# First places of runs by DRAM as a 123rd row of the rank product, and ScalarE's sort comparisons 22 places ahead of their scatters

## The chip, the cores and the metric

One core of a Trainium2 chip runs the whole program in one launch. The metric is the device time of one execution in microseconds. Besides the timed runs there is one execution with a profile; its trace carries every instruction of the engines TensorE (PE, with its weight loads PEld), VectorE (DVE), ScalarE (ACT) and GpSimd (POOL), and the DMAs that SP and the others issue.

## The reference

A layer of a graph network on 6,250 nodes of 128 features with 206,250 edges. The edges' features are added up by the edge's source node, and the sums go through three small layers and a normalization:

```
edge_aggr = zeros(n, 128).at[src].add(edge_attr)
combined  = concat([x, edge_aggr, global], -1) @ W_c + b_c
h   = softplus(combined @ W1 + b1)
h   = softplus(h @ W2 + b2)
out = layernorm(x + h @ W3 + b3)
```

Nearly all of the work is the sum by node, `.at[src].add`: the edges come in no order of `src`.

## The kernel before

**Sort, scatter, sum.** The nodes are cut into 32 buckets of 196. The edges lie as 122 partitions (`PN`) by 1,692 columns, two columns to a pair: 846 pairs. The program (1) sorts each column's 122 edges by bucket with a product of a 0/1 matrix (`sort_hot`) and the edges' rows (`gather`, TensorE, line 1153), (2) copies the result from PSUM to `pairs` (`settle`, ScalarE, 1165), (3) scatters one pair of columns per indirect DMA into `rows_by` in DRAM (`scatter_row`, GpSimd, 1182), where each bucket has a room of its own, (4) loads full chunks of 128 rows back (`load`, SP), makes 0/1 matrices of them against the 196 nodes (`match`, VectorE, 990) and multiplies them with the rows (`product`, TensorE, 1013), and adds that to `sums_t` (`add`, VectorE, 1036). When all is summed, the node layers follow (`node_layers`, lines 1340 on).

**Positions.** To sort a column, each edge needs its slot: the first place of its bucket's run in the column, and its rank within the run. To scatter, each sorted pair needs its row in `rows_by`. `positions(g)` computes both for one of eight groups of pairs (`GROUPS`: 28, 72, 124, 124, 124, 128, 124, 122), in sets of 16 columns, and sets in batches of up to four. A set has four quads of four columns. By step: `count_set` (VectorE, 498) makes the 0/1 tile `pair_ib` (edge by bucket and column); `counted` (TensorE, 509) counts the runs; `even_set` (520); `evened` (TensorE, 527) sums the counts up to the first places; `started` (VectorE, 534 to 538) takes them out of PSUM, as float32 (`starts`) and as a bfloat16 copy (`starts_h`); `ranked` (TensorE, 557 and 559) makes the slots; `slot_set` (VectorE, 576) reduces them to `slot`. `ranked` is one product of the 122 x 122 constant `rank` with `pair_ib` (512 columns), and then four products, one per quad, that add the first places: `starts_h` broadcast over 122 columns against the identity. From group 5 on (`GAP`), a group's positions come in two parts, counts first, ranks and rows a group later (`split`).

**What sets the order.** Nothing is scheduled by the machine: each engine runs its instructions in the order in which the program emits them, and that order is a list of events sorted by a planned time. A scatter is planned every 1.3 us (`SCATTER`) from 24 us on; a piece of three pairs is compared 17.5 ahead of its first scatter (`COMPARED`), gathered 14 ahead and settled 10.5 ahead. Even pieces are compared by VectorE in one instruction (1137), odd pieces by ScalarE in seven: six times `Abs` (1140) and one `Relu` over all (1142), half a place apart, and these begin another `SPREAD` (2.0) earlier. Rows of edges are loaded 36 ahead. The steps of `positions` are spread evenly over 85% of the time of the group before (`at_step` numbers them; `APART` is 3). All of SP's DMAs, loads of rows, loads of chunks and the fills of `rows_by`, are one queue (`sync_dma`, line 293), and SP waits in it for whatever the next DMA waits for.

The few lines that matter most here:

```
def rank(k, at, t):
    at_step(at, (1, lambda t=t: ranked(t)))
    at_step(at + APART, (0, lambda t=t: slot_set(t)))
...
for j in range(2 * pieces[i][2] + 1):
    when(t - COMPARED - SPREAD + j * SCATTER / 2, lambda i=i: compare_next(i))
```

## Time and profile before

| | |
|---|---|
| timed runs, us | 1288.87, 1288.93, 1285.73; median 1288.87 |
| the profiled execution, us | 1289.92 |
| its span, first to last instruction, us | 1288.2 |
| granted TensorE clock, mean | 0.962 |
| scatters on GpSimd | 846, from 22.1 to 1127.0 us |
| sort products and sum products on TensorE | 3384 and 3516 rows of the trace |
| packets of all DMA queues | 381.96 MB, 297 GB/s |

The span of the profiled execution lies 1.7 us under its time; the rest is ahead of the first and behind the last instruction. A product of float32 data is one instruction of the program and two rows of the trace. A duration of a product in a row reaches from its start to its modelled end, and products overlap; the distance of two starts is what one costs. "<-" in a wait names what ended last before the waiting instruction could start.

### The profile page before, as it was taken

The page shows a single profiled execution, that of the slowest core. Times are in us where ns is not written, and L with a number is a line of the kernel's source. Part 1 is how long each engine was busy: PE and PEld are TensorE (multiplying, and loading weights), DVE is VectorE, ACT ScalarE, POOL GpSimd, SP SyncE. Part 2 cuts the span into 40 slices and gives each one's busy share as a digit, 9 for nine tenths or more (in the row PEclk, how much of TensorE's full clock was granted, in tenths as well). Part 3 has the DMA queues.
Part 4 walks back from the last instruction along what each step waited for, and adds up shares of the span by engine and source line. Part 5 has one row for each costly group of instructions (what it writes and reads, how often), then busy time and mean ns, then how long its engine had stood idle before and what let it go on. Part 6 is the DMA issues. An engine that isn't in the chain of part 4 may idle for free.

```text
span 1288.2 us, 26304 instructions
## 1 busy us (share of the span) xinstructions
PE 1167.7 (91%) x8617; PEld 1111.8 (86%) x8617; DVE 1027.6 (80%) x2260; ACT 1003.9 (78%) x2335; POOL 880.9 (68%) x915
## 2 busy tenths in 40 slices
PE   5778898888998998999899999999999999899893
PEld 5667788877988898989899999999999999898772
DVE  7868977888789977899878887789876767687784
ACT  5897987899687888977998888988899999403343
POOL 2777777777577776776777777777777777750334
PEclk9788998989999998999999999999999999999996
DMA  6789998899999997997999999999999999874421
GB/s 248 240 296 347 344 334 288 305 344 355 339 327 331 362 330 278 319 325 246 322 309 309 323 336 328 345 313 335 316 350 334 369 336 363 288 218 140 140 75 53
DMA packets 174636, 381.96 MB, mean 297 GB/s; under 512 B 27546, under 2 KB 118626, under 8 KB 160670
## 3 DMA queue, kind: packets, MB, share of 16 engines
q1 hardware_dynamic: 130751, 260.70, 61.2%
q0 software_dynamic: 41328, 115.65, 23.1%
q10 hardware_dynamic: 2415, 3.85, 0.9%
q8 instruction: 72, 1.18, 0.4%
q14 instruction: 70, 0.57, 0.1%
HBM read 242.47 MB, written 142.20 MB: 299 GB/s over the span
## 4 chain that ended last, share of the span: by engine, by line
PE 65%; DVE 12%; ACT 8%; DMA 7%; issue 4%; POOL 3%; SPq 0%; ACTq 0%; DVEq 0%; POOLq 0%
PE part L1013 37%; PE sorted L1153 21%; ACT pairs L1165 4%; DMA rows_by<-pairs,pair 4%; POOL rows_by L1182 3%; ACT sort_hot L1140 3%; DMA chunks<-rows_by 3%; DVE hot L990 2%; DVE past L727 1%; PE small L557 1%; PE small L559 1%; ACT sort_hot L1142 1%; DVE sort_hot L1137 1%; DVE sums_t L1036 1%; PE small L1395 1%
## 5 line engine op out<-in xcount | busy, mean ns | idle before, releaser
L1182 POOL DMA_INDIRECT rows_by<-pairs,pair x846 | 828.1, 979 | 298.3 <-issue 202.8
L1013 PE MATMUL part<-hot,chunks 128*128 128x196 f32 x3516 | 675.1, 335 | 13.2 <-DVE sums_t L1036 9.9
L1165 ACT COPY pairs<-sorted 64x387 f32<-64x387 f32 (+2 forms) x1144 | 542.6, 474 | 118.8 <-PE sorted L1153 95.7
L1013 PEld LDWEIGHTS part<-hot,chunks 128*128 128x128 f32 x3516 | 582.0, 193 | 21.9 <-DVE sums_t L1036 11.3
L1153 PE MATMUL sorted<-rows,sort_hot 122*128 122x129 f32 x3384 | 498.5, 288 | 44.5 <-ACT sort_hot L1142 32.0
L1153 PEld LDWEIGHTS sorted<-rows,sort_hot 122*128 122x128 f32 x3384 | 457.6, 199 | 53.5 <-ACT sort_hot L1142 36.3
L990 DVE TENSOR_TENSOR hot<-chunks,both_ps 128x784 f32<-128x784 f32 (+3 forms) x541 | 426.1, 809 | 9.2 <-DMA chunks<-rows_by 9.0
L1140 ACT ACTIVATE sort_hot<-plain,slot 122x128 f32<-122x128 f32 x840 | 292.8, 394 | 18.6 <-PE sorted L1153 6.3
L1036 DVE TENSOR_TENSOR sums_t<-sums_t,part 128x392 f32<-128x392 f32 (+1 forms) x262 | 143.5, 548 | 134.0 <-PE part L1013 133.0
L1137 DVE TENSOR_TENSOR sort_hot<-slot,both_ps 122x768 f32<-122x768 f32 x143 | 134.5, 940 | 1.9 <-PE sorted L1153 1.0
L1142 ACT ACTIVATE sort_hot<-sort_hot 122x768 f32<-122x768 f32 x143 | 118.6, 830 | 3.9
L1437 POOL TENSOR_SCALAR y<-y,mv,rs 128x128 f32<-128x128 f32 x40 | 31.1, 785 | 93.8 <-DVE rs L1425 93.5
L576 DVE TENSOR_REDUCE slot<-small 122x16 f32<-122x512 f32 (+2 forms) x109 | 72.9, 668 | 21.5 <-PE small L559 20.7
L1367 ACT ACTIVATE away<-sorted,z_bias 128x512 f32<-128x512 f32 (+2 forms) x13 | 8.5, 656 | 72.9 <-PE sorted L1357 72.9
L498 DVE TENSOR_TENSOR pair_ib<-pair_block,plain 122x512 bf16<-122x512 bf16 (+2 forms) x157 | 63.4, 411 | 0.2
L557 PE MATMUL small<-pair_ib,half 122*122 122x512 bf16 (+2 forms) x109 | 43.3, 398 | 7.6 <-DVE slot L576 7.5
L742 PEld LDWEIGHTS <-past 128*128 128x128 f16 x424 | 25.4, 100 | 17.9 <-DVE past L727 12.7
L727 DVE TENSOR_TENSOR past<-both_ps,starts 128x512 f16<-128x512 f32 (+1 forms) x61 | 39.8, 664 | 1.2 <-PE small L742 0.9
L742 PE MATMUL small<-jump,past 128*128 128x56 f16 (+3 forms) x424 | 29.4, 190 | 11.8 <-DVE past L727 8.4
L559 PEld LDWEIGHTS <-starts_h 128*122 128x122 bf16 x236 | 25.3, 148 | 11.9 <-issue 7.7
L1114 ACT COPY rows<-pair_i 122x16 f32<-122x16 f32 x106 | 22.2, 209 | 17.0 <-DMA rows<-in_edge 16.4
L727 DVE TENSOR_TENSOR past<-both_ps,starts_late 128x512 f16<-128x512 f32 (+2 forms) x49 | 32.3, 661 | 0.0
(163 smaller groups left out, 515.6 us busy)
## 6 DMA issues: line engine op xcount, KB each, us to landing
rows<-in_edge SPq DMA_DIRECT2D x105, 1032.0 KB
chunks<-rows_by SPq DMA_DIRECT2D x362, 136.0 KB
chunks<-rows_by SPq DMA_DIRECT2D x203, 204.0 KB
chunks<-rows_by SPq DMA_DIRECT2D x75, 272.0 KB
rows_by<-pairs,pair POOLq DMA_INDIRECT x846
rows_by<-fill SPq DMA_DIRECT2D x10, 1249.5 KB
rows_by<-fill SPq DMA_DIRECT2D x10, 714.0 KB
chunks<-rows_by SPq DMA_DIRECT2D x13, 408.0 KB
```

The costliest lines, as they stand in the source:

```text
L498: nc.vector.tensor_tensor(ib, cols.unsqueeze(2).to_broadcast([PN, m, SB, QUAD]), bucket_at[:PN].unsqueeze(1).to_broadcast([PN, m, SB, QUAD ...
L576: nc.vector.tensor_reduce(to, of, axis=mybir.AxisListType.X, op=ALU.max)
L727: nc.vector.tensor_tensor(past[:, :, a:b], twice_ps[:KB].unsqueeze(1).unsqueeze(1).to_broadcast([KB, 2, b - a, P // 2]), own["starts"][:, ...
L990: nc.vector.tensor_tensor(hot[:, q - a:q - a + m], chunks[j][:, lo:hi + 1:step, D:W].to_broadcast([P, m, BL]), iota_ps.unsqueeze(1).to_bro ...
L1013: nc.tensor.matmul(part[:, b - base_of[v], :], t[:, place_in(j, q), :D], hot[:, q - a], start=first, stop=last)
L1036: nc.vector.tensor_add(here, here, of)
L1137: return [lambda: nc.vector.tensor_tensor(hot[:PN, :2 * m], slot[:PN, at:at + 2 * m].unsqueeze(2).to_broadcast([PN, 2 * m, P]), slot_ps[:P ...
L1140: return [lambda j=j: nc.scalar.activation(hot[:PN, j], by_slot[:PN], AF.Abs, bias=slot[:PN, at + j:at + j + 1], scale=-1.0) for j in rang ...
L1142: for j in range(2 * m)] + [lambda: nc.scalar.activation(hot[:PN, :2 * m], hot[:PN, :2 * m], AF.Relu, bias=1.0, scale=-1.0)]
L1153: nc.tensor.matmul(out[:, j, :], hot[:PN, at], rows_at[col // LOAD_COLS][:PN, col % LOAD_COLS, :], start=True, stop=True)
L1165: nc.scalar.copy(sets_at[i][64 * n:64 * n + 64, lo:lo + m, h, :W], out[64 * h:64 * h + 64, :m, :])
L1182: s = nc.gpsimd.indirect_dma_start(out=dst, out_offset=bass.IndirectOffsetOnAxis(ap=at, axis=0), in_=rows[:, j].rearrange("p a b -> p (a b ...
```

## The change

**The first places.** In groups 2 to 7 (`rowed`: from `ROWED` = 2 on) the four products by which `ranked` added the first places are gone. `pair_ib` has a 123rd partition, the constant `rank` a 123rd row of ones, and the rank product runs over 123 rows: whatever stands in row 122 of `pair_ib` is added to every slot of that bucket and column. To get the first places into that one row, `evened` makes one more product per batch that puts them with quads on partitions (up to 16 x 128), `started` copies that to SBUF as `starts_rows` (in place of the copy `starts_h`) and writes it to a DRAM tensor of the group, and `starts_row` reads, for each set, four quads of it as one row of 512 values into `pair_ib`. The write is at step 9 of a batch as `started` was; in groups 2 to 4 the read is at step 16 and the rank product at 22 in place of 15, and a batch of n sets takes 10n steps in place of 8n. In groups 5 to 7 the read stands where `count_set` stands in the second part, three steps ahead of the rank product. Counts and first places of a batch lie closer together in PSUM, so that the new product has room.

**The comparisons.** `SPREAD` is 4.5 in place of 2.0, so that ScalarE's part of the comparisons is planned 22 ahead of the scatter. The pool of `sort_hot` has four buffers in place of three, that of the matches (`hots`) five in place of six.

The core of the diff:

```diff
-GAP = 5
+GAP, ROWED = 5, 2
-SHARE, SPREAD = 2, 2.0
+SHARE, SPREAD = 2, 4.5
-    t["rank"] = MARK * (k == f) + (f > k)
+    t["rank"] = MARK * (k == f) + (f > k) + (k == PN)
+    rows_of = {g: dram.tile([2 * (s1 - s0) // QUAD, KB], BF16, name=f"starts{g}")
+               for g, (s0, s1) in enumerate(groups) if g >= ROWED}
-    hots = ctx.enter_context(tc.tile_pool(name="hots", bufs=6))
+    hots = ctx.enter_context(tc.tile_pool(name="hots", bufs=5))
-        sort_p = phase.enter_context(tc.tile_pool(name="sort", bufs=3))
+        sort_p = phase.enter_context(tc.tile_pool(name="sort", bufs=4))
-        rank_h = rank_h[:PN, :PN]
+        rank_h = rank_h[:PN + 1, :PN]
-            split = g >= GAP
+            split, rowed = g >= GAP, g >= ROWED
-                ib = pairs_in.tile([PN, STEP // QUAD, SB, QUAD], BF16, name="pair_ib", bufs=5)[:, :m]
+                ib = pairs_in.tile([PN + 1, STEP // QUAD, SB, QUAD], BF16, name="pair_ib", bufs=5)[:, :m]
...
                 for k, by in enumerate((lower_h, through_h, lower_or_all_h)):
-                    nc.tensor.matmul(small_of["counts", ts][:KB, (1 + k) * P:(1 + k) * P + n], by,
+                    a = SPAN + (1 + k) * BATCH * STEP // QUAD
+                    nc.tensor.matmul(small_of["counts", ts][:KB, a:a + n], by,
                                      own["evens"][:, at], start=True, stop=True)
+                if rowed:
+                    nc.tensor.matmul(small_of["counts", ts][:n, P:P + KB], own["evens"][:, at],
+                                     lower_h, start=True, stop=True)
...
-                nc.vector.tensor_copy(own["starts_h"][:, at], small[:, 1, :n])
+                if not rowed:
+                    nc.vector.tensor_copy(own["starts_h"][:, at], small[:, 1, :n])
+                    return
+                rows_h = per.tile([BATCH * STEP // QUAD, KB], BF16, name="starts_rows", bufs=2)
+                nc.vector.tensor_copy(rows_h[:n], small_of["counts", ts][:n, P:P + KB])
+                sync_dma(rows_of[g][at], rows_h[:n])
+
+            def starts_row(t):
+                q0, n = t // QUAD, per_set(t)
+                sync_dma(in_set[t][PN:PN + 1].rearrange("p q b c -> p (q b c)"),
+                         rows_of[g][q0:q0 + n].rearrange("(o q) k -> o (q k)", o=1))
...
-                nc.tensor.matmul(pr, rank_h, in_set.pop(t)[:, :, :NB, :], start=True, stop=False)
+                k = PN + rowed
+                nc.tensor.matmul(pr, rank_h[:k], in_set.pop(t)[:k, :, :NB, :], start=True, stop=rowed)
+                if rowed:
+                    return
                 for q in range(per_set(t)):
...
                     at_step(base + 4 * k, (6, lambda t=t: count_set(t)))
+                    if rowed and not split:
+                        at_step(base + gap + 16 + 5 * k, (2, lambda t=t: starts_row(t)))
                     if not split:
-                        rank(k, base + gap + 5 * APART + 5 * k, t)
+                        rank(k, base + gap + (22 if rowed else 5 * APART) + 5 * k, t)
...
-                base += (4 if split else 8) * n
+                base += (4 if split else 10 if rowed else 8) * n
...
                     at_step(4 * n, (6, lambda t=t: count_set(t)))
+                    at_step(4 * n, (7, lambda t=t: starts_row(t)))
                     rank(n, 4 * n + APART, t)
```

How the instructions stand now, at three places.

ScalarE in group 3, from the comparisons of one odd piece (the `Abs` and the `Relu` into one `sort_hot`) to the copies of that piece's sorted pairs (into `pairs1`). Before, the comparisons into `sort_hot_4449`:

```order
L1140 ACTIVATE sort_hot_4449<-plain_60,slot_2025 122x128 x2
L1165 COPY pairs5_113<-sorted_4423 64x3x129 x2
L1140 ACTIVATE sort_hot_4449<-plain_60,slot_2025 122x128 x2
L1114 COPY rows_4279<-pair_i_114 122x16
L1140 ACTIVATE sort_hot_4449<-plain_60,slot_2025 122x128
L1165 COPY pairs5_113<-sorted_4444 64x3x129 x2
L1140 ACTIVATE sort_hot_4449<-plain_60,slot_2025 122x128
L1142 ACTIVATE sort_hot_4449<-sort_hot_4449 122x768
L1165 COPY pairs0_108<-sorted_4474 64x3x129 x2
L1165 COPY pairs0_108<-sorted_4501 64x3x129 x2
L1140 ACTIVATE sort_hot_4549<-plain_60,slot_2025 122x128 x2
L1165 COPY pairs1_109<-sorted_4513 64x3x129 x2
```

And now the same piece, into `sort_hot_4334`:

```order
L1167 ACTIVATE sort_hot_4334<-plain_60,slot_1999 122x128 x3
L1192 COPY pairs4_118<-sorted_4318 64x3x129 x2
L1167 ACTIVATE sort_hot_4334<-plain_60,slot_1999 122x128 x3
L1192 COPY pairs5_119<-sorted_4346 64x3x129 x2
L1169 ACTIVATE sort_hot_4334<-sort_hot_4334 122x768
L1141 COPY rows_4217<-pair_i_120 122x16
L1192 COPY pairs5_119<-sorted_4366 64x3x129 x2
L1192 COPY pairs0_114<-sorted_4383 64x3x129 x2
L1167 ACTIVATE sort_hot_4434<-plain_60,slot_1999 122x128 x3
L1192 COPY pairs0_114<-sorted_4408 64x3x129 x2
L1167 ACTIVATE sort_hot_4434<-plain_60,slot_1999 122x128 x3
L1192 COPY pairs1_115<-sorted_4436 64x3x129 x2
```

Between the last step of the comparisons and the first copy of their own piece stood four copies and two comparisons of the next piece; now there are six copies, six comparisons and a copy of nodes.

TensorE in group 1, where the positions of group 2 are made, from the first batch's last product of first places to its first rank product (into `small` from `pair_ib`). Before:

```order
L527 MATMUL small<-evens,half 128x16
L1153 MATMUL sorted<-rows,sort_hot 128x129 x6
L557 LDWEIGHTS half
L557 MATMUL small<-pair_ib,half 122x512
L559 LDWEIGHTS starts_h
L559 MATMUL small<-half,starts_h 122x128
```

And now:

```order
L531 MATMUL small<-evens,half 128x16
L534 LDWEIGHTS evens
L534 MATMUL small<-half,evens 16x128
L1180 MATMUL sorted<-rows,sort_hot 128x129 x9
L579 LDWEIGHTS half
L579 MATMUL small<-pair_ib,half 122x512
L1180 MATMUL sorted<-rows,sort_hot 128x129 x3
```

Nine products of the sort stand between the two in place of six, and the four products of `starts_h` behind the rank product are gone.

SP in group 3, where the positions of group 4 are made (`starts_81` is that group's DRAM tensor). Before:

```order
L293 DMA chunks<-rows_by 128x408
L293 DMA chunks<-rows_by 128x272 x5
L293 DMA rows<-in_edge 128x2064
L293 DMA rows_by<-fill 112x3x952
L293 DMA rows<-in_edge 128x2064
```

And now:

```order
L295 DMA chunks<-rows_by 128x408
L295 DMA chunks<-rows_by 128x272 x5
L295 DMA starts_81<-starts_rows 16x128
L295 DMA pair_ib<-starts_81 1x512
L295 DMA rows<-in_edge 128x2064
L295 DMA pair_ib<-starts_81 1x512 x2
L295 DMA rows_by<-fill 112x3x952
L295 DMA pair_ib<-starts_81 1x512
L295 DMA rows<-in_edge 128x2064
L295 DMA starts_81<-starts_rows 16x128
```

The batch's write and its four reads stand between the loads of chunks and of edge rows, which wait behind them; the next batch's write follows.

More of the change, by code (lines that the diff above doesn't have):

```diff
@@ L182 @@
     assert NB * STEP <= 4 * P and KB <= P
-    assert 2 * BATCH * STEP + SPAN <= 4 * P and BATCH * STEP // QUAD + SPAN <= P
+    assert 2 * BATCH * STEP + SPAN <= 4 * P and 5 * BATCH * STEP // QUAD + SPAN <= P
     W = D + 1
@@ L482, in opened @@
                     own["starts"] = per.tile([KB, 2, Q_MAX], F32, name="starts" + late, bufs=max(2, deep))
-                    own["starts_h"] = per.tile([KB, Q_MAX], BF16, name="starts_h" + late, bufs=deep)
+                    if not rowed:
+                        own["starts_h"] = per.tile([KB, Q_MAX], BF16, name="starts_h", bufs=1)
                     own["earlier"] = per.tile([KB, 2, Q_MAX], F32, name="earlier" + late, bufs=deep)
@@ L526, in evened, with by_kind @@
                 for k, by in enumerate((lower_h, through_h, lower_or_all_h)):
-                    nc.tensor.matmul(small_of["counts", ts][:KB, (1 + k) * P:(1 + k) * P + n], by,
+                    a = SPAN + (1 + k) * BATCH * STEP // QUAD
+                    nc.tensor.matmul(small_of["counts", ts][:KB, a:a + n], by,
                                      own["evens"][:, at], start=True, stop=True)
+                if rowed:
+                    nc.tensor.matmul(small_of["counts", ts][:n, P:P + KB], own["evens"][:, at],
+                                     lower_h, start=True, stop=True)
+            def by_kind(small):
+                at = slice(SPAN, SPAN + 4 * BATCH * STEP // QUAD)
+                return small[:KB, at].rearrange("k (a q) -> k a q", a=4)
             def started(ts):
@@ L532, in started @@
                 n = at.stop - at.start
-                small = small_of["counts", ts][:KB].rearrange("k (a q) -> k a q", a=4)
+                small = by_kind(small_of["counts", ts])
                 nc.vector.tensor_scalar(own["starts"][:, 0, at], small[:, 1, :n], 0.0, None,
@@ L542, in odd_set @@
                 n = at.stop - at.start
-                small = small_of.pop(("counts", ts))[:KB].rearrange("k (a q) -> k a q", a=4)
+                small = by_kind(small_of.pop(("counts", ts)))
                 odd_i = per.tile([KB, 2, BATCH * STEP // QUAD], I32, name="odd_i")[:, :, :n]
@@ L813, in positions @@
                     at_step(base + 4 * k, (6, lambda t=t: count_set(t)))
+                    if rowed and not split:
+                        at_step(base + gap + 16 + 5 * k, (2, lambda t=t: starts_row(t)))
                     if not split:
-                        rank(k, base + gap + 5 * APART + 5 * k, t)
+                        rank(k, base + gap + (22 if rowed else 5 * APART) + 5 * k, t)
                 for k, step in enumerate((counted, even_set, evened, started, odd_set)):
                     at_step(base + gap + APART * k, (-k, lambda step=step, ts=ts: step(ts)))
-                base += (4 if split else 8) * n
-                end = base - (4 if split else 8) * n + gap + 4 * APART
+                base += (4 if split else 10 if rowed else 8) * n
+                end = base - (4 if split else 10 if rowed else 8) * n + gap + 4 * APART
             at_step(end + 1, (-1, all_sets))
```

5 lines of the change are left out of this document (3 added, 2 removed).

## The prediction

> **What bounds the kernel now.** I read the page's sums and the median first, then busy time by stretch, then what GpSimd's scatter waits for, then the other waits and the chain. The profiled execution took 1289.92 us, 1.05 above the median of the three timed runs (1288.87); its span is 1288.2. The sum below is made against 1289.92, and 1.05 is taken off at the end.
>
> ```profile
> PE 1167.7 (91%) x8617; PEld 1111.8 (86%) x8617; DVE 1027.6 (80%) x2260; ACT 1003.9 (78%) x2335; POOL 880.9 (68%) x915
> ```
> ```profile
> 64.00:400.00 336.00, 288.47 (x2325) 272.41 (x2324) 275.55 (x682) 284.67 (x669) 247.17 (x252) 0.94 0.93 328
> 400.00:640.00 240.00, 221.97 (x1756) 215.63 (x1754) 208.63 (x479) 201.21 (x472) 176.99 (x181) 0.97 0.90 314
> 640.00:1110.00 470.00, 468.01 (x3446) 462.73 (x3447) 361.24 (x604) 420.49 (x990) 358.04 (x368) 1.00 0.96 329
> ```
>
> By the whole, TensorE looks like the bound (91%). By stretch it isn't that plain. The scatters tell more:
>
> ```profile
> L1182 POOL DMA_INDIRECT rows_by<-pairs,pair x846: 971/972/1407, 22.1 to 1127.0; - x170
> ...
>   issue: 202.8, 663
>   DMA rows_by<-pairs,pair: 33.0, 78
>   ACT pairs L1165: 23.9, 51
>   DVE much L642: 20.5, 1
>   ACT sort_hot L1140: 7.3, 20
>   ACT sort_hot L1142: 3.7, 12
> ```
>
> A scatter takes 0.972 us, and 0.306 us (202.8/663) pass before the next even when nothing is waited for: a pace of 1.278. From 640 to 1110 us 368 scatters at that pace are 470 us, the whole stretch: there GpSimd is at its floor and nothing else in the kernel can shorten it. From first to last start 845 paces are 1079.9 us and took 1104.9, so 25 us in all are lost, all of it ahead of 640. Beyond the 0.306 that each pays anyway, 83 waits for ScalarE cost 34.9 - 25.4 = 9.5 us and 78 waits for a DMA 33.0 - 23.9 = 9.1; lengthened scatters make most of the rest. (The 20.5 is ahead of the first one.) What follows the last scatter hangs on it:
>
> ```profile
> 1119.28 7.08 DMA chunks<-rows_by
> ...
> 1127.95 28.81 PE part L1013 x162
> ```
>
> The last chunks can't be loaded before their rows are scattered, and from the last scatter (1128) to the end of the span TensorE has 160 us of sums and node layers, in an order that the change leaves alone. So the time is the scatters' end plus a fixed tail, and an edit is worth what it gives or takes of those 25 us.
>
> **The removed products.** 373 weight loads and products of the first places (four a set) go in groups 2 to 7.
>
> ```profile
> 331.77 0.17 DVE L538 CAST starts_h<-small 128x16 bf16<-128x16 f32 x1
> ...
> 334.81 0.38 PE L557 MATMUL small<-pair_ib,half 122*122 122x512 bf16 x1
> ...
> 335.02 0.39 PE L559 MATMUL small<-half,starts_h 128*122 128x128 bf16 x4
> ```
> ```profile
> L559 PE MATMUL small<-half,starts_h x236: 217/218/314, 11.2 to 398.1; 128*122 128x128 bf16 x118
> ```
>
> Four of them end 0.39 us after the first starts and one takes 0.218, so they follow each other at (0.39 - 0.218)/3 = 0.057 us: 373 are 21.3 us of TensorE. The Trainium skill (TensorE: Matmul & The Clock Gate, Back-to-back issue gap) gives about 81 ns for each weight load and product at 128 columns in a stream, which would make 30 us; the trace is lower and decides. Credit on the path: none directly, because GpSimd sets the pace; it is room for what follows. One more product a batch (24) gives back 24 x 0.057 = 1.4 us. The row 123 adds no columns to the rank product.
>
> **ScalarE's earlier comparisons.** Ahead of 640 us TensorE stands still for 65.5 us (336 - 288.5 = 47.5, then 240 - 222 = 18), and half of that has one cause:
>
> ```profile
> PEld sorted L1153 <- ACT sort_hot L1142: 33.7, 22, 2.4
> PE sorted L1153 <- ACT sort_hot L1142: 29.9, 21, 2.2
> ```
> ```profile
> L1165 ACT COPY pairs<-sorted 64x387 f32<-64x387 f32 (+2 forms) x1144 | 542.6, 474 | 118.8 <-PE sorted L1153 95.7
> ...
> L1140 ACT ACTIVATE sort_hot<-plain,slot 122x128 f32<-122x128 f32 x840 | 292.8, 394 | 18.6 <-PE sorted L1153 6.3
> ```
>
> (The two waits are of one stall, seen by weight loads and products.) The order puts six copies and six comparisons between a piece's last step and its own first copy where four copies and two comparisons stood. At 0.474 and 292.8/840 = 0.349 us the lead grows from 2.6 to 4.9 us, by 2.3; the longest stall was 2.4. So nearly all of these 30 us go. Late next are the copies themselves, which now stand behind more comparisons; ScalarE is 84% busy to 640 (284.67 + 201.21 of 576), so they find room. GpSimd waited for ScalarE 9.5 us beyond its pace: I take all of it, -9.5; the bounds are 0 (the copies come as late as before) and -25 (every scatter on time). The fourth buffer of comparisons is what lets them start. The buffer taken from the matches costs nothing while VectorE is two units ahead; at the end four ahead still fit in five:
>
> ```profile
> PEld part L1013 <- DVE hot L990: 1.1, 3, 0.4
> ```
>
> Bound: 0 to 2 us.
>
> **The trip by DRAM.** Per batch VectorE's copy of the rows (24 of them, as long as the 0.17 that it replaces, within a tenth), a write on SP, its landing, then a read per set (96) and its landing, and only then the rank product, in TensorE's order, with the sort's products behind it and, through ScalarE's copies, the scatter. No small DMA between DRAM and SBUF within the loop is in the trace. The nearest rows, from an idle queue, from the tail and from a loaded one:
>
> ```profile
> 0.75 2.96 DMA pair_i<-in_src
> ```
> ```profile
> 1182.51 2.08 DMA chunks<-rows_by
> ```
> ```profile
> 278.72 8.11 DMA chunks<-rows_by
> ```
> ```profile
> 72.33 0.28 PE L527 MATMUL small<-evens,half 128*128 128x16 bf16 x3
> ...
> 72.89 0.16 DVE L538 CAST starts_h<-small 128x16 bf16<-128x16 f32 x1
> ```
> ```profile
> 1103.39 1.34 PE sorted L1153 x12
> ```
>
> From the batch's product (72.33) to the end of the copy (73.05) is 0.72 us. With 2.96 for each trip the chain is 0.72 + 5.92 = 6.6 us; with 2.08, 4.9; with one trip behind a loaded queue, 0.72 + 8.11 + 2.96 = 11.8. I take 6.6, since SP has just waited when it writes and little is queued. The Trainium skill (DMA: Bandwidth & Descriptors, Anatomy of one DMA) puts about 2.0 us of fixed cost on every DMA, most of it the receipt from the target memory, which would make the chain 4.7, an estimate; the trace's 2.08 agrees with it.
>
> The cover: in groups 3 and 4 the copy preceded the rank product by 334.81 - 331.77 = 3.04 us for 6 steps of the plan; it is now 13 steps, each 0.9 of before (224 in place of 200 in a group), so 5.9, and 0.72 for what precedes the copy: 6.6. That just covers. In group 2 there is no work of the sums yet; between the batch's product and the rank product TensorE has nine of the sort's products, 18 of the trace's rows at 1.34/12 = 2.0 us, and its own 0.28: 2.3. So 4 batches x 4.3 = 17 us of stall in group 2, none in the others. Room for it:
>
> ```profile
> 64.00:128.00 64.00, 49.43 (x416) 44.76 (x414) 49.47 (x143) 56.44 (x133) 48.75 (x51) 0.89 0.89 320
> ```
>
> 14.6 us idle and 16 sets x 4 x 0.057 = 3.6 us of removed work: 18.2 against 17. It fits, barely; I charge the scatters +2.5, with 0 and +12 as ends. In groups 5 to 7 the write is a whole group ahead, and each read stands three steps ahead of its product. They are tightest in group 5:
>
> ```profile
> 569.79 0.38 PE L557 MATMUL small<-pair_ib,half 122*122 122x512 bf16 x1
> ...
> 625.29 0.38 PE L557 MATMUL small<-pair_ib,half 122*122 122x512 bf16 x1
> ```
>
> These are the first and the last of the 16 rank products of group 5: 55.5/15 = 3.7 us for four steps, 2.8 for three, against a trip of 2.96. That is 16 x 0.2 = 3 us of stall, and 16 x 0.228 = 3.6 of removed work pay for it: 0, with +8 as the end if each trip takes 0.5 us more.
>
> **SP's queue.** 120 more issues:
>
> ```profile
> L293 SPq DMA_DIRECT2D rows<-in_edge x106: 327/378/3285, 1.2 to 1083.9; - x106
> ```
> ```profile
> SPq L293 <- PE part L1013: 400.9, 175, 7.7
> SPq L293 <- PE sorted L1153: 200.7, 43, 20.3
> ```
> ```profile
> ACT rows L1114 <- DMA rows<-in_edge: 16.4, 7, 3.9
> ...
> DVE hot L990 <- DMA chunks<-rows_by: 9.0, 9, 2.5
> ```
>
> At 0.378 us they take 45 us, and 24 writes hold SP until VectorE's copy, 12 of them a landing more (12 x 2.96 = 36 us); row and chunk loads stand behind. SP waits 602 us for TensorE to free buffers, which hides it: those loads would have stood still anyway, and VectorE and ScalarE wait for loads only 25 us in all. Without that cover the worst is a load late by what SP ran ahead, up to the 7.7 of its longest usual wait, at some of 24 places. Taken: 0; ends 0 and +8.
>
> Sum: 1289.9 - 9.5 + 2.5 = 1282.9; less 1.05, 1282.
>
> **The rivals.**
>
> *The DRAM trip is slow (slower).* If one landing in each of groups 2 to 4 is as in the loaded row, the chain is 11.8: 4 x 9.5 + 8 x 5.2 = 80 us of stall from 64 to 400 us, against 47.5 idle there and 48 x 0.228 = 10.9 of removed work. 21 us reach the scatters, less the 9.5 won: 1289.9 + 11.7 - 1.05 = 1300.5. With a landing L for each trip the stall is 24 L - 53, and it decides from L = 5.2 us on (72 us: the room of 58, the 9.5 and a measurable 4). For it: DMA is 0.93 busy in that stretch. Against it: SP is idle ahead of each trip, so its own queue is short.
>
> *The waits change places (no change).* ScalarE is as full as before; if GpSimd's 9.5 us return as waits for copies that stand behind comparisons, or group 2 takes them, the time is 1289.9 - 1.05 = 1289, within 1286 to 1292. For it: 9.1 of the 25 us are waits for DMAs, which this change touches at best by accident. Against it: TensorE loses 30 us of stalls and 20 us of work, so copies come earlier.
>
> *TensorE was the bound after all (much faster).* Then its net 21.3 - 1.4 = 20 us fall through: 1269.9 - 1.05 = 1269. By the Trainium skill's 81 ns (the section named above) it would be 28 us and 1261. For it: 468 of 470 us busy from 640 on. Against it: the scatters are at their floor there, and the scatters' whole loss is 25.
>
> **How the numbers follow.** Forecast 45% (1277 to 1287 by itself: 0 to -25 of gain cut to what ScalarE holds, with the two small ends), slow trip 25%, waits change places 20%, TensorE bound 10%. About 0.3% (3.9 us: under 1285 or over 1292.7) is what a measurement can tell from no change. Faster: 0.43 of the forecast's case and the 0.10: 0.53. Same: the 0.20 and 0.02: 0.22. Slower: 0.25. The range 1270 to 1299 leaves out most of the 0.10 and about half of the slow trip's 0.25, so 0.2.
>
> **What would show it.** Right: the scatters' last start near 1120 instead of 1127 with no wait for ScalarE over the pace; the stalls of the sort's products on the comparisons below 8 us; a first rank product of a batch in group 2 waiting 3 to 5 us for a DMA and none elsewhere over 2; the tail still 160 us. Wrong: rank products that wait for their DMA in groups 3 to 7, loads that land late after each write, or a last scatter at 1127 or later.

## The result, and the profile after

| | before | after |
|---|---|---|
| median of the timed runs, us | 1288.78 (1285.73 to 1288.97, 6 runs) | 1361.33 (1352.26 to 1367.20, 6 runs) |
| profiled execution / its span, us | 1289.92 / 1288.2 | 1364.49 / 1362.7 |
| last scatter's start, us | 1127.0 | 1200.1 |
| granted TensorE clock, mean | 0.962 | 0.938 |

The changed kernel takes 1.056 times as long (95% interval 1.052 to 1.060): 72.6 us more, where 7 us less was forecast and 1299 was the upper end.

The sums of the page, and its chain by engine:

```profile
PE 1163.3 (85%) x8268; PEld 1101.7 (81%) x8268; DVE 1031.6 (76%) x2260; ACT 980.3 (72%) x2335; POOL 882.0 (65%) x915
...
PE 52%; DMA 19%; DVE 13%; issue 5%; ACT 5%; POOL 3%; SPq 2%; ACTq 0%; DVEq 0%; POOLq 0%
```

No engine does more work than before by more than 4 us (VectorE, 1027.6 to 1031.6); each is busy for a smaller share of a longer span. So the time is waiting. Where it was lost, the scatters tell first:

```profile
L1209 POOL DMA_INDIRECT rows_by<-pairs,pair x846: 971/972/1452, 22.3 to 1200.1; - x170
...
  issue: 195.8, 640
  ACT pairs L1192: 121.7, 112
...
  DMA rows_by<-pairs,pair: 14.4, 39
```

From the first to the last start 845 paces of 1.278 us are 1079.9 and took 1177.8: 98 us are lost in place of 25, and that is the 73 us. Behind the last scatter 162.6 us follow, before it was 161.2: the tail is nearly what it was. GpSimd waits 121.7 us for ScalarE's copies where it waited 23.9. ScalarE in turn, and TensorE, by the list of waits:

```profile
ACT pairs L1192 <- PE sorted L1180: 212.5, 162, 13.5
...
PE small L579 <- DMA pair_ib<-starts: 84.0, 26, 14.9
DVE slot L600 <- PE small L579: 78.8, 26, 12.8
...
PEld sorted L1180 <- ACT pairs L1192: 33.3, 37, 2.7
...
PE sorted L1180 <- ACT pairs L1192: 19.3, 24, 2.6
```

The new wait is the second line: 26 rank products stand 84.0 us for the first places to land, up to 14.9 us each. TensorE takes its products in the program's order, so the sort's products stand behind them, ScalarE has nothing to copy, and GpSimd nothing to scatter. No wait of the sort's products on ScalarE's comparisons is left in the list; they wait for its copies now, though.

How much of the standing still reaches the end is seen by busy time between the same scatters (those that before started at 63.5, 400.2, 640.6 and 1110.4 us). After, and then before:

```profile
63.70:448.70 385.00, 285.83 (x2100) 266.89 (x2101) 266.31 (x638) 271.92 (x655) 247.79 (x252) 0.86 0.83 287
448.70:702.50 253.80, 224.02 (x1737) 215.18 (x1736) 219.53 (x517) 199.19 (x482) 178.14 (x181) 0.97 0.84 295
702.50:1183.50 481.00, 463.99 (x3317) 459.06 (x3318) 361.51 (x603) 409.73 (x987) 358.01 (x367) 0.98 0.93 322
```
```profile
63.50:400.20 336.70, 289.17 (x2329) 273.11 (x2329) 276.22 (x683) 285.03 (x671) 247.67 (x253) 0.94 0.93 328
400.20:640.60 240.40, 221.78 (x1755) 215.44 (x1754) 209.03 (x480) 201.60 (x474) 177.29 (x181) 0.97 0.90 314
640.60:1110.40 469.80, 468.40 (x3449) 463.12 (x3450) 361.04 (x604) 420.00 (x989) 357.88 (x367) 1.00 0.95 329
```

TensorE's idle time (the stretch less its busy time) was 47.5, 18.6 and 1.4 us and is 99.2, 29.8 and 17.0: 78.4 us more, while its busy time fell by 5.5 only. Idle time lay free before and was not used up: the new stalls came on top of it.

Why a landing takes so long shows in SP's queue. First the pieces of the chain of waits that are trips by DRAM, in group 1, where group 2's positions are made (start, duration from issue to landing):

```profile
70.46 1.34 DMA starts<-starts_rows
...
72.53 7.37 DMA pair_ib<-starts
...
86.18 1.30 DMA starts<-starts_rows
...
87.50 1.27 DMA pair_ib<-starts
...
98.25 5.34 DMA starts<-starts_rows
...
103.66 10.52 DMA pair_ib<-starts
```

The second batch finds a free queue: 1.30 and 1.27 us, less than half of the 2.96 that the forecast took (that row carried 818 KB). The third takes 5.34 and 10.52. What stands ahead of a slow one is plain at 401 us (group 3; the timeline of SP's issues and the rank products, start, duration, and in brackets the wait):

```profile
401.47 0.38 SPq L295 DMA_DIRECT2D rows<-in_edge  x1
...
401.89 0.29 SPq L295 DMA_DIRECT2D pair_ib<-starts  x1
402.22 0.33 SPq L295 DMA_DIRECT2D rows_by<-fill  x1
...
402.60 0.33 SPq L295 DMA_DIRECT2D pair_ib<-starts  x1
...
407.71 0.68 PE L579 MATMUL small<-pair_ib,half 123*122 123x512 bf16 x1 [5.40 <-DMA pair_ib<-starts]
...
411.95 0.68 PE L579 MATMUL small<-pair_ib,half 123*122 123x512 bf16 x1 [2.26 <-DMA pair_ib<-starts]
```
```profile
rows<-in_edge SPq DMA_DIRECT2D x105, 1032.0 KB
...
rows_by<-fill SPq DMA_DIRECT2D x10, 1249.5 KB
```

The first read (1 KB) was issued behind 1,032 KB of edge rows, the second behind these and 1,249.5 KB of fill. At the 287 GB/s of that stretch the bytes ahead are 3.7 and 8.1 us; the products started 5.8 and 9.3 us after the issues. A 1 KB transfer waits for the megabytes ahead of it.

The trace's records of DMA packets show the same for all reads. A read is one packet, which itself took about 0.05 us; 95 of the 96 could be matched to their issues. The packet started between 0.85 and 9.82 us after the issue, 4.03 in the median (5.29 and 8.41 for the two reads above). When a read was issued, 1.05 MB (median) of SP's earlier transfers had not started; when its packet started, nothing of these was left (median). A straight line through the 95 reads is 0.86 us and 3.1 us more for each MB ahead (correlation 0.97).

The Trainium skill (DMA: Bandwidth & Descriptors, Queues, rings and completion order) says that each DMA engine takes one queue's descriptors in the order of its ring, and goes round between queues; the trace agrees with the first half here (1.05 MB ahead at the issue, nothing left at the start), and run 5 tries the second.

By groups, with the distance from the start of the product ahead of a rank product to its own start, less the shortest such distance of that kind, these stalls sum to 23.2, 11.4, 39.6, 6.5, 1.3 and 15.7 us for the positions of groups 2 to 7: 97.6, where before it is 7.0. Of the 84.0 us in the list of waits, 20.6 lie ahead of the issue of the read that was waited for, and 63.4 behind it: most of it is the trip, and a part is SP issuing late.

### The profile page after: what moved, and what is told of

It is laid out like the page before. It is cut to its first block, busy times and chain, and to the rows that moved or that the text cites. A ratio compares the mean times of both kernels' runs of the same rounds, so it can differ in the third digit from the quotient of the medians.

```text
span 1362.7 us, 25746 instructions
## 1 busy us (share of the span) xinstructions
PE 1163.3 (85%) x8268; PEld 1101.7 (81%) x8268; DVE 1031.6 (76%) x2260; ACT 980.3 (72%) x2335; POOL 882.0 (65%) x915
## 4 chain that ended last, share of the span: by engine, by line
PE 52%; DMA 19%; DVE 13%; issue 5%; ACT 5%; POOL 3%; SPq 2%; ACTq 0%; DVEq 0%; POOLq 0%
PE part L1040 31%; PE sorted L1180 17%; DMA pair_ib<-starts 7%; DMA rows_by<-pairs,pair 4%; POOL rows_by L1209 3%; DVE hot L1017 3%; DMA chunks<-rows_by 3%; ACT pairs L1192 2%; SPq L295 2%; DMA starts<-starts_rows 2%; DMA rows<-in_edge 2%; DMA rows_by<-fill 2%; PE small L579 1%; DVE sort_hot L1164 1%; ACT sort_hot L1167 1%
## 5 line engine op out<-in xcount | busy, mean ns | idle before, releaser
L1040 PE MATMUL part<-hot,chunks 128*128 128x196 f32 x3516 | 681.8, 338 | 23.1 <-DVE sums_t L1063 10.5
L1040 PEld LDWEIGHTS part<-hot,chunks 128*128 128x128 f32 x3516 | 590.9, 195 | 65.0 <-issue 36.8
L1180 PE MATMUL sorted<-rows,sort_hot 122*128 122x129 f32 x3384 | 494.6, 287 | 21.2 <-ACT pairs L1192 19.3
L1180 PEld LDWEIGHTS sorted<-rows,sort_hot 122*128 122x128 f32 x3384 | 462.3, 199 | 59.3 <-ACT pairs L1192 33.3
L1167 ACT ACTIVATE sort_hot<-plain,slot 122x128 f32<-122x128 f32 x840 | 280.2, 392 | 9.5 <-DVE slot L600 5.8
L579 PE MATMUL small<-pair_ib,half 123*122 123x512 bf16 (+3 forms) x109 | 48.2, 443 | 91.5 <-DMA pair_ib<-starts 84.0
L579 PEld LDWEIGHTS <-half 123*122 123x122 bf16 (+1 forms) x109 | 16.3, 150 | 38.8 <-DMA pair_ib<-starts 38.7
## 6 DMA issues: line engine op xcount, KB each, us to landing
rows_by<-fill SPq DMA_DIRECT2D x10, 1249.5 KB
```

The costliest lines, as they stand in the source:

```text
L579: nc.tensor.matmul(pr, rank_h[:k], in_set.pop(t)[:k, :, :NB, :], start=True, stop=rowed)
L1040: nc.tensor.matmul(part[:, b - base_of[v], :], t[:, place_in(j, q), :D], hot[:, q - a], start=first, stop=last)
L1167: return [lambda j=j: nc.scalar.activation(hot[:PN, j], by_slot[:PN], AF.Abs, bias=slot[:PN, at + j:at + j + 1], scale=-1.0) for j in rang ...
L1180: nc.tensor.matmul(out[:, j, :], hot[:PN, at], rows_at[col // LOAD_COLS][:PN, col % LOAD_COLS, :], start=True, stop=True)
```

## The experiments

Times are medians; a ratio is to the kernel before on the same chip (1286.37 us beside the first four, 1288.22 beside the next four, 1287.72 beside the last four), with its 95% interval. The three groups of four were run on three chips, whose kernels before differ by up to 1.9 us, so a difference between runs of two groups is good to about 2 us.

**1. The comparisons alone.** Before with only

```diff
-SHARE, SPREAD = 2, 2.0
+SHARE, SPREAD = 2, 4.5
-    hots = ctx.enter_context(tc.tile_pool(name="hots", bufs=6))
+    hots = ctx.enter_context(tc.tile_pool(name="hots", bufs=5))
-        sort_p = phase.enter_context(tc.tile_pool(name="sort", bufs=3))
+        sort_p = phase.enter_context(tc.tile_pool(name="sort", bufs=4))
```

> Only ScalarE's earlier comparisons, the fourth buffer of comparisons and the fifth (not sixth) of matches; first places as before. Theory A (this part does what was forecast, the loss is all in the trip by DRAM): 1282, with the waits of the sort's products on ScalarE's comparisons gone. Rival B (the new order on ScalarE takes part in the loss, its copies coming late behind more comparisons): 1295 or more, with GpSimd waiting for ScalarE's copies. Third case: no change, 1286 to 1292.

Measured: 1282.97 us, ratio 0.9974 (0.9959 to 0.9989): 3.4 us less. Its waits:

```profile
POOL rows_by L1182 <- DMA rows_by<-pairs,pair: 28.9, 69, 2.3
PE sorted L1153 <- ACT pairs L1165: 28.3, 32, 4.7
...
POOL rows_by L1182 <- ACT pairs L1165: 22.5, 62, 1.4
```

The same in the kernel before:

```profile
PE sorted L1153 <- ACT pairs L1165: 8.8, 12, 3.6
```

The waits on comparisons (29.9 us of it ahead of 640) are gone, and most of them came back one step later: the sort's products wait 28.3 us for ScalarE's copies, before 8.8. GpSimd's wait for these copies hardly changed (23.9 to 22.5). So the forecast of this part (theory A) comes out in time. This kernel is faster than the kernel before and than the changed one.

**2. The row alone**: after with `SPREAD = 2.0` and the pools of before.

> Only the row by DRAM; comparisons and buffers as before. Theory A: 1361 or more, about the changed kernel plus what the earlier comparisons give (1365 to 1370). Rival B: clearly less than the changed kernel, under 1345.

Measured: 1365.99 us, ratio 1.0598 (1.0562 to 1.0635). The loss is the row's, all of it, as theory A has it. The comparisons may be worth some 5 us within it (1361.3 against 1366.0), but that lies inside the spread of either kernel.

**3. Both trips, waited for by nobody.** In `ranked` of after:

```diff
-                k = PN + rowed
+                k = PN
```

> The changed kernel, but in groups 2 to 7 the rank product runs over 122 rows and leaves the first places out of the slots; all 120 DMAs are issued as before, and nobody waits for the reads. Theory A1 (TensorE waits for reads that land late behind loads in SP's queue: 98 us of stalls ahead of rank products): close to the forecast, 1280 to 1300. Rival A2 (the writes hold SP, and the loads behind them are late, whoever waits for the reads): 1330 to 1360.

Measured: 1315.27 us, ratio 1.0231 (1.0202 to 1.0261), between the two theories. The slots of groups 2 to 7 lack their first places in this kernel, and in runs 7, 9, 10 and 12. 46 us go with the rank products' wait, and 29 us stay though no product needs the data. What is late now:

```profile
DVE pair_ib L501 <- DMA pair_ib<-starts: 37.5, 9, 9.9
```

The 0/1 tile can't be filled anew while a read into its row 122 is under way: the late landing holds VectorE in place of TensorE.

**4. The row in groups 5 to 7 only**, where a trip has most time: `ROWED = 5`.

> The changed kernel with the row only in groups 5 to 7, where the write is a group ahead. Groups 2 to 4 have 74 of the 98 us of stalls. Theory A1: the scatters of groups 0 to 4 end as early as with the comparisons alone, and what is left are the stalls of groups 5 to 7 (23 us of TensorE, mostly one of 11 us for the scatters): 1285 to 1300. Rival A2 (holding SP): the twelve writes of groups 5 to 7 stand in the same stretch, so half of the loss stays, 1315 to 1330.

Measured: 1298.13 us, ratio 1.0073 (1.0045 to 1.0100), inside theory A1's range. Without the row it is 1283.0 (run 1), so 15 us are lost in the groups that were forecast at 0, with +8 as the end. The other 63 us belong to groups 2 to 4.

**5. A queue of its own.** Both DMAs issued by ScalarE:

```diff
-                sync_dma(rows_of[g][at], rows_h[:n])
+                nc.scalar.dma_start(rows_of[g][at], rows_h[:n])
...
-                sync_dma(in_set[t][PN:PN + 1].rearrange("p q b c -> p (q b c)"),
+                nc.scalar.dma_start(in_set[t][PN:PN + 1].rearrange("p q b c -> p (q b c)"),
```

> The changed kernel with its 120 small DMAs issued by ScalarE instead of SP. Theory C (the trips are long because they stand behind the loads of SP's queue, and SP's loads behind them): rank products wait under 25 us in all, SP is held no more, and what is left is ScalarE held by the writes and their landings: 1290 to 1310. Rival D (the DMA engines are so loaded that a small DMA is slow from any queue): landings of 5 to 8 us as before, ScalarE held by them as well, 1340 or more.

Measured: 1329.04 us, ratio 1.0316 (1.0282 to 1.0350): 32 us of the 73 come back, between theory C and rival D.

```profile
PE small L579 <- DMA pair_ib<-starts: 42.6, 13, 5.5
```

The rank products' waits halve (84.0 to 42.6 us, the longest 14.9 to 5.5). So SP's queue makes half of these waits. The other half stays on a queue that carries little else, with the DMA engines 0.87 busy from 64 to 448 us.

The packet records tell what is left. Only 3.3 of the 42.6 us lie ahead of the read's issue, so it isn't ScalarE's issuing. The reads' packets start 3.02 us after the issue in the median (4.03 on SP's queue), at most 7.23. Where over 1.5 MB of SP's loads had not started at the issue, it is 4.07 us in the median (25 reads), with 0.70 MB of these loads still not started then; on SP's queue it was 6.68 us (13 reads), with nothing left. With the engines going round between queues, as the Trainium skill has it, a read should not have to wait for all of the other queue's loads; the trace agrees in that it overtakes a part of them. But a queue of its own is far from a free trip while the other queue is full. Why it still takes 3 us is not shown.

**6. More lead on SP's queue.** Reads at step 30 and rank products at 48 (after: 16 and 22), 16 steps to a set, and in groups 5 to 7 reads six steps ahead:

```diff
-                        at_step(base + gap + 16 + 5 * k, (2, lambda t=t: starts_row(t)))
+                        at_step(base + gap + 30 + 5 * k, (2, lambda t=t: starts_row(t)))
...
-                        rank(k, base + gap + (22 if rowed else 5 * APART) + 5 * k, t)
+                        rank(k, base + gap + (48 if rowed else 5 * APART) + 5 * k, t)
```

> The changed kernel, SP's queue, with more steps between: in groups 2 to 4 the read 21 steps behind the write (7 before) and the rank product 18 behind the read (6 before), a batch of n sets taking 16n steps; in groups 5 to 7 the read three steps behind the set's 0/1 tile and the rank product six behind the read. Theory C: waits of rank products under 15 us, SP held only for VectorE's copy at the writes, 1285 to 1300. Rival E (it is the holding of SP that costs, whatever the lead): 1310 or more.

Measured: 1337.91 us, ratio 1.0382 (1.0342 to 1.0421). Three times as many steps stand between read and product, though each is shorter (a batch takes 16 steps to a set where it took 10), and still:

```profile
PE small L579 <- DMA pair_ib<-starts: 34.7, 9, 6.4
```

Theory C, under 15 us of waits and 1285 to 1300, fails; the time is that of rival E. But with 34.7 us of waits left, the run doesn't tell how much of it is the holding of SP.

**7. The writes alone.** No reads, and the rank product over 122 rows as in run 3.

> The changed kernel with the 24 writes and without the 96 reads; the rank product runs over 122 rows and leaves the first places of groups 2 to 7 out of the slots. Against the kernel with unread rows (1315) it tells the writes' share from the reads'. If the writes hold SP (each waits for VectorE's copy): 1305 to 1315. If the reads do (each waits for a write's landing or for VectorE's 0/1 tile, and VectorE waits for late reads): 1280 to 1288.

Measured: 1297.70 us, ratio 1.0077 (1.0052 to 1.0103). What SP waits for:

```profile
SPq L295 <- DVE pair_ib L501: 51.9, 6, 13.2
...
SPq L295 <- DVE odd_i L568: 43.3, 5, 14.1
...
SPq L295 <- DVE starts_rows L553: 20.2, 2, 12.8
...
SPq L295 <- DVE odd_i L567: 13.1, 2, 9.9
```

and what waits for the loads behind:

```profile
ACT rows L1138 <- DMA rows<-in_edge: 27.0, 9, 6.0
...
DVE hot L1014 <- DMA chunks<-rows_by: 23.4, 13, 6.4
```

15 times a write stands at the head of SP's queue until VectorE has come so far, 128.5 us in all and up to 14.1 at once, and the loads of rows and chunks stand behind it. In run 9, without the writes, none of these lines is over 0.6 us. The time lies between the two cases that were expected, and above run 9 by 11.9 us. How it gets there is shown for a part only: of the 12.3 us between the two profiled executions 5.5 are the scatters' loss (28.5 against 23.0), and 6.4 the tail behind the last scatter (163.6 against 157.2), which no write touches.

**8. Own queue and more lead**: runs 5 and 6 together.

> Both: ScalarE's queue and the longer leads. Theory C: no wait of a rank product over 1 us, SP free, ScalarE held only for VectorE's copy at 24 writes and by 120 issues of about 0.3 us: 1280 to 1295, at best as good as the comparisons alone (1283). If the issues or holds on ScalarE cost the scatters: 1300 or more.

Measured: 1323.21 us, ratio 1.0269 (1.0231 to 1.0307): the second case. The stalls at rank products fall to 15.0 us by the distances, and the time hardly follows:

```profile
PEld sorted L1180 <- ACT pairs L1192: 64.2, 61, 8.2
...
PE sorted L1180 <- ACT pairs L1192: 46.9, 46, 7.9
```

ScalarE's issues of the writes now wait for VectorE, which shows as waits of what it does next:

```profile
ACT sort_hot L1167 <- DVE pair_ib L501: 12.1, 4, 6.5
...
ACT pairs L1192 <- DVE odd_i L568: 8.6, 3, 3.8
```

Its copies stand behind, and the sort's products wait for these 46.9 us, up to 7.9 at once (19.3 in after, 28.3 with the comparisons alone). A write that waits for VectorE now stands ahead of ScalarE's own work, where it stood ahead of SP's loads. How much of the 35 us over before this makes is not shown.

**9. No DMA at all**: after without the write and the reads, the rank product over 122 rows; the extra product, VectorE's copy and the longer step plan stay.

> The changed kernel without any of the 120 DMAs; its products, copies and step numbers as changed, the rank product over 122 rows, the first places of groups 2 to 7 left out of the slots. If the stretched steps and the rest of the program cost nothing: 1278 to 1286, like the comparisons alone (1283) or better by the removed products. If the steps themselves cost: 1290 or more, and then part of the 1298 with writes alone isn't the writes'.

Measured: 1285.78 us, ratio 0.9984 (0.9957 to 1.0011). Its loads:

```profile
ACT rows L1137 <- DMA rows<-in_edge: 13.4, 7, 4.6
...
DVE hot L1013 <- DMA chunks<-rows_by: 11.3, 8, 5.1
```

Everything in the change but the DMAs and the 123rd row costs nothing that can be measured. (A rank product lasts 0.382 us in the median in after, most of them over 123 rows, and 0.379 before, over 122.) The removed products bring nothing that can be measured either: 1.9 us less than before, the comparisons alone 3.4 less.

**10. One read per set from a constant, unread.** No write; row 122 is read from the constants `half_in`, which needs no wait for data, and the product takes 122 rows:

```diff
-                sync_dma(rows_of[g][at], rows_h[:n])
...
-                sync_dma(in_set[t][PN:PN + 1].rearrange("p q b c -> p (q b c)"),
-                         rows_of[g][q0:q0 + n].rearrange("(o q) k -> o (q k)", o=1))
+                sync_dma(in_set[t][PN:PN + 1].rearrange("p q b c -> p (q b c)"), half_in[:1, :n * KB])
...
-                k = PN + rowed
+                k = PN
```

> The same 96 DMAs from the input constant, now into the 123rd row of the set's tile as changed, but read by nobody; no writes. What it adds to the loose ones is the tie to the tile: SP waits for VectorE's 0/1 tile ahead of a read, and VectorE for a late read ahead of the tile's next use. Expected 10 to 20 us over the loose ones if this is the reads' share (the kernel with unread rows was 17.6 over the one with writes alone); none if it is the wait for the write's landing.

Measured: 1300.96 us, ratio 1.0098 (1.0073 to 1.0123): 14.6 us over the loose ones (run 12), as expected of the tie to the tile.

```profile
DVE pair_ib L501 <- DMA pair_ib<-in_half: 21.8, 8, 8.1
```

Of the two sides of the tie it is this one: SP waits for VectorE's 0/1 tile only 2.6 us in all.

**11. The same read, waited for**: run 10 with the product over 123 rows.

> The same from the input constant, and the rank product reads the 123rd row and so waits for it; no writes, so one trip in place of two (the slots get the constant's values in place of first places). Theory C says that the second trip, the write's landing ahead of the read, makes much of the waits: rank products wait under 40 us here (98 in the changed kernel) and the time is 1305 to 1330. If one trip behind SP's loads is enough for the whole loss: 1345 or more.

Measured: 1335.04 us, ratio 1.0364 (1.0341 to 1.0388).

```profile
PE small L577 <- DMA pair_ib<-in_half: 52.3, 20, 6.8
```

One landing that a product waits for costs 34 us more than one that no product waits for, with no write ahead of it. Both cases that were expected miss: the products wait 52.3 us in place of under 40, and the time lies between 1330 and 1345.

**12. The same 96 small DMAs, tied to nothing**: SP copies the constant into the groups' DRAM tensors, at the same steps.

```diff
-                sync_dma(in_set[t][PN:PN + 1].rearrange("p q b c -> p (q b c)"),
-                         rows_of[g][q0:q0 + n].rearrange("(o q) k -> o (q k)", o=1))
+                sync_dma(rows_of[g][q0:q0 + n].rearrange("(o q) k -> o (q k)", o=1), half_in[:1, :n * KB])
```

> As the kernel without DMAs, and on SP, at the places of the 96 reads, 96 DMAs of the same size from an input constant into DRAM that nobody reads: no tie to any engine. It prices issue and SP's places in flight (each of SP's DMAs takes the next of eight semaphores and waits for the DMA eight before it). If that is free: within 4 us of the kernel without DMAs. If it counts: 8 to 20 us more.

Measured: 1286.34 us, ratio 0.9990 (0.9970 to 1.0010): 0.6 us over run 9. Issuing 96 more DMAs on SP, and the places that they take among those under way, cost nothing that can be measured.

The runs as two ways from no DMA to the change, us:

| step | time | added |
|---|---|---|
| no DMA (9) | 1285.8 | |
| 96 DMAs, tied to nothing (12) | 1286.3 | 0.6 |
| tied to the 0/1 tile (10) | 1301.0 | 14.6 |
| waited for by the rank product (11) | 1335.0 | 34.1 |
| the data by DRAM: a write ahead of each four (after) | 1361.3 | 26.3 |

| step | time | added |
|---|---|---|
| no DMA (9) | 1285.8 | |
| writes, read by nobody (7) | 1297.7 | 11.9 |
| reads, waited for by no product (3) | 1315.3 | 17.6 |
| waited for by the rank product (after) | 1361.3 | 46.1 |

## Why the prediction was wrong

**The trip by DRAM is the step that failed**: "I take 6.6, since SP has just waited when it writes and little is queued". That SP has waited says nothing of what it issues next. Loads of rows, chunks and fills go out just ahead of the small transfers: 1.05 MB in the median of the reads, 1 to 2.3 MB in the example above, and a landing behind them takes 5 to 10.5 us. On a free queue it takes 1.3, so 2.96 was not too low for a free queue; it was the wrong state of the queue. (The 2.0 us that the prediction takes from the Trainium skill, DMA: Bandwidth & Descriptors, Anatomy of one DMA, is told there of DMAs that GpSimd issues; on SP's free queue 1.27 to 1.34 us were measured, and the measurement decides.) The order told it: the pieces of SP's queue shown with the change have an edge-row load or a fill directly ahead of two of the four reads. The stall was 23 us in group 2, where 17 was forecast, and 11, 40 and 16 in groups 3, 4 and 7, where none was. The nearest row was the one that only the rival used (8.11, from the loaded queue).

**The slow trip was among the rivals, with the right stall and the wrong price.** It forecast 80 us of stalls in groups 2 to 4, and 74.2 were measured there, with 23.5 in groups 5 to 7, where it had none: 90.6 more than before (97.6 less 7.0). It then let 58 vanish in "room": TensorE's idle time of 47.5 us and the removed work. Of 90.6 us of stall 78.4 appeared as added idle time and 72.6 in the time. A reading that fits the two rows: idle time in short waits for ScalarE and for buffers can't be used up by one long stall, because those who make TensorE wait later get their input from it and don't run ahead while it stands. No run shows this by itself. With no room the rival would have read 1289.9 + 80 - 9.5 - 1.05 = 1359; that this is so near to 1361 is in part luck, since it counts 80 us of stall where 90.6 came, and all of them as lost where 72.6 were. It would have decided from (53 + 9.5 + 3.9)/24 = 2.8 us a landing on, under the 2.96 that the forecast itself took.

**SP's queue, "Taken: 0; ends 0 and +8"**: 12 us for the writes alone (run 7). The path that was named and dismissed takes part: chunk loads are late for VectorE by 23.4 us in place of 11.3 in run 9 (7.4 in run 12), row loads for ScalarE by 27.0 in place of 13.4 (but 21.2 in run 12, at no cost in time). In the two profiles it accounts for the 5.5 us of scatters' loss at most. In sum the cover was there: SP's waits for TensorE's buffers fell by 126 us in run 7 (441.1 in place of 567.3), as much as the 128.5 of the holds. But it is a sum over the whole kernel, and a hold of 14 us lies at one place. The issues themselves were rightly taken at nothing (run 12).

**A cost that was not in the sum**: a read into a row of a tile ties the whole tile. VectorE waits for the landing before it fills the tile anew, 15 us without any product that needs the data (run 10).

**The comparisons**: mechanism right, size wrong. The waits on them went, as forecast, and 3.4 us came (run 1) in place of 9.5. "Late next are the copies themselves... so they find room" is the step: GpSimd still waits 22.5 us for the copies, and the copies are what the sort's products wait for now. That is most of the rival in which the waits change places.

**The removed products** were credited with nothing on the path, rightly within what can be measured (run 9); with that the rival in which TensorE was the bound falls. Even as room they were smaller than counted. In run 9, over the same scatters, busy time is

```profile
63.80:396.00 332.20, 285.58 (x2145) 263.74 (x2144) 271.96 (x673) 277.71 (x669) 248.44 (x252) 0.92 0.94 332
396.00:639.00 243.00, 217.64 (x1694) 208.92 (x1692) 211.56 (x484) 195.22 (x470) 178.34 (x181) 0.97 0.89 310
639.00:1108.70 469.70, 464.76 (x3336) 459.07 (x3337) 361.90 (x604) 409.44 (x987) 357.71 (x367) 0.99 0.95 329
```

967.98 us in place of 979.35: 11.4 less, where 20 was counted.

**The frame held**: the pace of 1.278, and the time as the scatters' loss plus a tail. The tail was 157 to 164 us in the fourteen profiles, with no order to it, so it blurs differences of a few us but not the large ones. The large losses come ahead of 700 us, and once more where group 7's positions are made, in after (10 us at 967) and in runs 2, 4 and 11.

**What stays open**: in run 5 half of the rank products' waits remain on a queue without large transfers. They lie behind the reads' issues, so ScalarE's issuing late isn't it; how the loads of the other queue delay a small transfer is not shown. Run 8 still loses 35 us with few stalls at rank products, and half of run 7's 12 us lies in the tail; both are explained in part only. That the row pays nowhere is not shown either: a version whose writes are placed where VectorE's copy is surely done, on a queue of small transfers with a group's lead, wasn't tried. By run 9 it could at best reach the comparisons' time.

## What to carry to other kernels

Price a small transfer that an engine waits for by the bytes that stand ahead of it in its queue at its issue (here 0.86 us and 3.1 us for each MB until its packet starts), not by the latency of a free one; a queue of its own shortens this, but did not end it here. Price a DMA that waits for an engine by what stands behind it at that place. Take stalls in an in-order queue as lost unless a row shows that the idle time that they are to replace would end at the same place: here 72.6 of 90.6 us reached the time. And ask first whether what the trip removes is on the path: here 373 products were worth nothing that could be measured (run 9), and the DMAs that save them cost 1361.3 - 1285.8 = 75.5 us.

## What was not expected of the hardware

- The granted clock fell together with the stalls. In the first stretch, over the same scatters, it was 0.94 before, 0.92 with the products removed and nothing else late (run 9), and 0.86 in after, and in one stretch of after

```profile
384.00:448.00 64.00, 44.07 (x291) 42.32 (x290) 33.98 (x72) 32.10 (x79) 28.94 (x30) 0.81 0.71 231
```

it was 0.81. The Trainium skill (TensorE: Matmul & The Clock Gate, Part 1) has the array's clock halved after an idle window of about 3.4 us, and back after a busy one; rows with stalls of 5 to 15 us and a clock of 0.81 agree with it. Part of the work that was removed seems to be given back in slower products: in the first stretch after has 170 rows fewer by the removed products less the new ones, 9.7 us at 0.057, and 59 rows fewer of other work, and still its busy time fell by 3.3 only.
- A 1 to 4 KB transfer between DRAM and SBUF landed 1.27 to 1.34 us after its issue on a free queue, and a 1 KB one 10.52 us after it on a loaded one.
- A small transfer on a queue of its own still started 3.02 us after its issue in the median, 4.03 behind the loads of SP's queue (run 5).
